# Keeping h and u in the column order of the weights, in a masked-attention kernel

## The chip, the cores and the metric

The kernel runs on one core of a Trainium2 chip. The metric is the time of one execution in device microseconds. The kernel before takes 635.86 us, the median of three runs (634.95 to 635.87). One further execution was profiled; it took 631.83 us.

## The reference

A graph of 2708 nodes has features x of [2708, 1024] and a sparse 0/1 matrix adj with about four ones in a row. All is float32.

```
h = maximum(layernorm(x), 0)
q = h @ W_q.T + b_q;  k = h @ W_k.T + b_k;  v = h @ W_v.T + b_v
z = (q @ k.T) / 32 * adj
z = where(z == 0, -10000, z)
out = x + relu(softmax(z) @ v)
```

With so few ones in a row, the kernel gathers the few rows of h that a node needs and never forms k, v or the whole of z. It uses q·k = (h M + b')·h with M = W_q.T W_k / 32, and softmax(z) @ v = u @ W_v.T + b_v with u the weighted sum of gathered rows of h.

## The kernel before

**Layouts.** The host hands W_q and W_k over with their columns permuted: position 8 m + c of a row holds input feature 128 c + m. This is the weights' column order, (m c). x, and so h, q and u, lie in natural order, (c m). A block c of 128 features is contiguous in natural order; in the weights' order its elements are 8 floats, or 32 bytes, apart. `a_tile` (L465) takes such a block out of a row of W_q as a stationary operand.

**The work in stages.** There are 22 tiles of 128 rows; the last has 20.

- To about 104 us, TensorE forms M by a Strassen-like scheme in blocks (`term`, L473 to 478). The sums lie in PSUM banks X, Y and Z, and ACT (`evicted`, L490) or VectorE (`joined`, L494, two instructions a bank) writes them to M. Both read the bank with a stride and write pieces of 64, so that M's columns are in natural order. `ts_of_m` (L438) then forms four differences T of M's quadrants on VectorE, in two parts of the columns.
- Beside it, rows of x are loaded by SP, VectorE (`bn_stats`) or ACT (`moments`) takes their statistics, GpSimd the root (L259 to 267), and ACT normalises them in place (`apply`, L276). ACT issues the store to h_dram (L283) and GpSimd adds them to hsum (L285, L298). VectorE and ACT search the rows of adj for the ones, and a counting sort orders the nodes by their number of ones. After that, work goes by sorted tiles.
- Ten units of two tiles each form q (units 0 to 9, to about 347 us), and ten units of two tiles plus a single last tile (8) form the output. A unit is seven products of 512-wide quadrants (`multiply`, L1044), each four matmuls of [128x128] by [128x512] (L1010).
- The stationary operands of a unit are blocks of the transposed rows. For rows of h, and for two tiles of u that are still in SBUF, TensorE transposes them against an identity (`half_turned`, L415), eight 128x128 blocks a tile, and ACT copies the banks out (L718). For all other rows of u, the row goes through DRAM: ACT copies u to a buffer v with pieces reordered (L944) and issues its store to u_dram, SP loads it back in four pieces of a quarter of the partitions (`by_quarters`), and VectorE turns the 32x32 blocks (`faces`, L705).
- `attention` (L959) is a stream of VectorE steps: a score for each gathered row (L863), the softmax weights, and the weighted sum u (L923). From unit 5 on it is advanced between the products of the units, by an amount of nominal time for each product (`share`, L1239 to 1242), less where the next unit has faces to turn.

**Order.** VectorE runs in the order of the program throughout, ACT until unit 4, GpSimd until unit 2. The rest is placed by the scheduler of the language.

**Row buffers.** `row_tile` (L211) hands out seven buffers of [128, 1024] in turn: for x (and h in place), for gathered rows of h, for u, for v and for rows of u loaded back. Tiles 15 to 17, and 19's companions 20 and 21, use buffers of other kinds.

```
def faces(dst, xt, lo, hi):
    return nc.vector.transpose(dst.rearrange("p c (g r) -> p g c r", r=QP),
                               xt.rearrange("p (g c r) -> p g c r", g=QUADS, r=QP)[:, :, lo:hi])
```

Of the kernel before, what the change touches and what calls it, by code (L numbers as in the profile page):

```python
# [10 lines left out]
FT = mybir.dt.float32  # L11
# [54 lines left out]
def tile_preln_masked_attention(  # L66
# [203 lines left out]
    def apply(first, only=range(4)):  # L270

        group, xs, r = normed[first]
        for i in only:
            if i < len(group):
                n = tiles[group[i]][1]
                nc.scalar.activation(xs[i][:n], xs[i][:n], AF.Relu, bias=r[:n, 4, i:i + 1], scale=r[:n, 3, i:i + 1])  # L276

# [132 lines left out]
    def half_turned(xt, s):  # L410

        pt = psum.tile([P, 4, P], FT, tag="tp", name="pt")
        for c in range(4):
            k = s * 4 + c
            nc.tensor.transpose(pt[:, c, :], xt[:, k * P:(k + 1) * P], ident)  # L415
        return pt
# [29 lines left out]
    with tc.tile_pool(name="w", bufs=1, side="left") as wp:  # L446
# [33 lines left out]
        def place(g, half, i):  # L480

            dst = M[:, g, :, i, :].rearrange("q j (c p) -> q j c p", p=P)
            pw = P // NH
            return dst[:, :, :, half * pw:(half + 1) * pw]

        def taken(bank):
            return bank.rearrange("q (p j c) -> q j c p", j=2, c=4)

        def evicted(bank, g, half, i):
            nc.scalar.activation(place(g, half, i), taken(bank), AF.Copy, scale=scale)  # L490

        def joined(bank, g, half, i):
            for j in range(2):
                nc.vector.scalar_tensor_tensor(place(g, half, i)[:, j], taken(bank)[:, j], scale,  # L494
                                               place(g, half, i)[:, j], op0=ALU.mult, op1=ALU.add)

# [89 lines left out]
        follow("i6.1-3")  # L586
        ts_of_m(0, 0)
        ts_of_m(1, 0, 1, 2, 3)
        follow("i7.0-1")
        for i in range(H):  # L590
            if i == 1:
                for half in range(NH):
                    ps = psum.tile([P, NB], FT, tag="acc", name="ps_v")
                    nc.tensor.matmul(ps, ones, acc_b[:, half * NB:(half + 1) * NB], start=True, stop=True)
                    pw = P // NH
                    nc.scalar.copy(bp_sb.rearrange("q (c p) -> q c p", c=DC)[:, :, half * pw:(half + 1) * pw],
                                   ps.rearrange("q (p c) -> q c p", c=DC))
                nc.vector.tensor_sub(bp_sb[:, NB:], bp_sb[:, NB:], bp_sb[:, :NB])
# [93 lines left out]

    faced = []

    def by_quarters(dst, rows):
# [7 lines left out]
    def faces(dst, xt, lo, hi):  # L703

        return nc.vector.transpose(dst.rearrange("p c (g r) -> p g c r", r=QP),  # L705
                                   xt.rearrange("p (g c r) -> p g c r", g=QUADS, r=QP)[:, :, lo:hi])

# [62 lines left out]
    banks_of = {0: banks_for(bp_sb)}  # L770
    ts_of_m(0, 1, 3, 2)
    follow("f8 k2 p7")
# [146 lines left out]
    def sums(t):  # L919
# [22 lines left out]
        if t in faced_tiles:  # L942
            v = row_tile(f"v_{t}")
            nc.scalar.copy(v.rearrange("p (a c r) -> p c a r", a=QUADS, r=QP),  # L944
                           u.rearrange("p (c a r) -> p c a r", a=QUADS, r=QP))
            nc.scalar.dma_start(u_dram[t * P:(t + 1) * P, :], v)
        elif near(t):
# [446 lines left out]
    with tc.If(some > 0):  # L1394
        with tc.tile_pool(name="mgen", bufs=1, side="right") as mgen:
# [6 lines left out]
            for c in range(DC):  # L1402
                mrow = mgen.tile([P, D], FT, tag="mrow", name="g_mrow", bufs=2)
                for h in range(NH):
                    ps = psum.tile([P, NB], FT, tag="acc", name="g_pm")
                    for o in range(DC):
                        nc.tensor.matmul(ps, weights_q[o].rearrange("o (p c) -> o c p", c=DC)[:, c, :],
                                         weights_k[o][:, h * NB:(h + 1) * NB], start=(o == 0), stop=(o == DC - 1))
                    pw = P // NH
                    nc.scalar.activation(mrow.rearrange("q (c p) -> q c p", c=DC)[:, :, h * pw:(h + 1) * pw],  # L1410
                                         ps.rearrange("q (p c) -> q c p", c=DC), AF.Copy, scale=scale)
                nc.sync.dma_start(m_dram[c // 4, :, :, c % 4, :].rearrange("j p w -> p j w"),
                                  mrow.rearrange("p (j w) -> p j w", j=2))
        with tc.tile_pool(name="big", bufs=1, side="right") as big, tc.tile_pool(
# [15 lines left out]
            for h in range(NH):  # L1430
                ps = psum.tile([P, NB], FT, tag="acc", name="g_c")
                nc.tensor.matmul(ps, ones, acc_c[:, h * NB:(h + 1) * NB], start=True, stop=True)
                pw = P // NH
                nc.vector.tensor_copy(c_sb.rearrange("q (c p) -> q c p", c=DC)[:, :, h * pw:(h + 1) * pw],
                                      ps.rearrange("q (p c) -> q c p", c=DC))
            bv_sb = big.tile([P, D], FT, name="bv_all")
# [3 lines left out]
            for t, (t0, n) in enumerate(tiles):  # L1440
                ht = gen.tile([P, D], FT, tag="ht", name="g_h")
                nc.sync.dma_start(ht[:n], h_dram[t0:t0 + n, :])
                for s in range(DC // 4):
                    pt = psum.tile([P, 4, P], FT, tag="tp", name="g_pt")
                    for c in range(4):
                        k = s * 4 + c
                        nc.tensor.transpose(pt[:, c, :n], ht[:n, k * P:(k + 1) * P], ident[:n, :n])
                    nc.vector.tensor_copy(hT[:, s * 4:(s + 1) * 4, t0:t0 + n], pt[:, :, :n])
            with tc.For_i(0, NT) as i:
# [5 lines left out]
                for k in range(DC):  # L1455
                    pt = psum.tile([P, 4, P], FT, tag="tp", name="g_ph")
                    nc.tensor.transpose(pt[:, 0, :], ht[:, k * P:(k + 1) * P], ident)
                    nc.vector.tensor_copy(qT[:, k, :], pt[:, 0, :])
# [22 lines left out]
                for k in range(DC):  # L1481
                    pt = psum.tile([P, 4, P], FT, tag="tp", name="g_pq")
                    nc.tensor.transpose(pt[:, 0, :], q[:, k * P:(k + 1) * P], ident)
                    nc.vector.tensor_copy(qT[:, k, :], pt[:, 0, :])
# [28 lines left out]
                for k in range(DC):  # L1513
                    pt = psum.tile([P, 4, P], FT, tag="tp", name="g_pu")
                    nc.tensor.transpose(pt[:, 0, :], u[:, k * P:(k + 1) * P], ident)
                    nc.vector.tensor_copy(qT[:, k, :], pt[:, 0, :])
# [54 lines left out]
```

## Time and profile before

| what | value |
|---|---|
| runs | 635.86 us median of 3 (634.95 to 635.87) |
| the profiled execution | 631.83 us |
| its span, from first to last instruction | 630.1 us |
| granted TensorE clock | 0.999 |
| TensorE matmul busy | 619.6 us |
| VectorE busy | 523.3 us |
| ACT busy | 288.4 us |
| GpSimd busy | 363.1 us |
| mean DMA rate | 289 GB/s |
| first matmul of the weights' product | 5.73 us |
| end of M, start of unit 0 | about 104 us |
| first face transpose | 347.9 us |

PE is TensorE's matmuls, PEld its loads of stationary operands (they run beside matmuls), DVE is VectorE, POOL is GpSimd. A group line names the line of the program, the engine, the operation, out<-in, shapes and count; then busy time and mean ns of one; then the idle time of the engine before it and what ended it. A line of a table of windows has the start and end of a stretch, its length, and then for each engine the busy time and the number of instructions, the granted clock, the share of DMA and GB/s. Matmuls are pipelined: a 128x512 matmul has two records of some 592 ns that begin 0.43 us apart.

### The profile page before, as it was taken

What the parts mean: (1) busy time and instruction counts of PE and PEld (TensorE: products, weight loads), DVE (VectorE), ACT (ScalarE), POOL (GpSimd) and SP (SyncE); (2) the same over time, 40 slices, a digit from 0 to 9 for tenths busy, and PEclk for the clock granted to TensorE, in tenths of its full rate; (3) what the DMA queues carried; (4) which work ended last, traced back from release to release, by engine and by line L of the source; (5) the groups of instructions that cost most, each with busy time, mean ns of one, the idle gap of its engine ahead of it and who ended that gap; (6) DMA issues with size and microseconds to landing.
All of it is one profiled execution on the core that took longest, in us unless ns stands there. A gap on an engine that the chain in (4) does not pass through costs nothing.

```text
span 630.1 us, 6067 instructions
## 1 busy us (share of the span) xinstructions
PE 619.6 (98%) x1579; PEld 310.3 (49%) x1579; DVE 523.3 (83%) x1022; ACT 288.4 (46%) x421; POOL 363.1 (58%) x394
## 2 busy tenths in 40 slices
PE   8999999999999999999999998999999999999996
PEld 5777766444444444454454443444444444444442
DVE  5999879997996664887988969999997999988741
ACT  3538985749677563343341333434342323343300
POOL 2649860885778177754561632757667477852241
PEclk9999999999999999999999999999999999999999
DMA  8999997688796439997489998899999999997481
GB/s 330 407 371 326 343 354 294 209 288 326 255 387 241 166 113 319 350 379 236 154 306 325 332 359 265 235 333 346 347 318 324 344 278 305 349 284 194 103 296 71
DMA packets 65088, 182.19 MB, mean 289 GB/s; under 512 B 9959, under 2 KB 20023, under 8 KB 64408
## 3 DMA queue, kind: packets, MB, share of 16 engines
q0 software_dynamic: 26656, 86.02, 43.4%
q1 hardware_dynamic: 31594, 71.53, 32.8%
q10 hardware_dynamic: 6798, 24.20, 9.8%
q8 instruction: 14, 0.23, 0.2%
q14 instruction: 26, 0.21, 0.1%
HBM read 146.70 MB, written 43.36 MB: 302 GB/s over the span
## 4 chain that ended last, share of the span: by engine, by line
PE 56%; DMA 17%; DVE 11%; issue 9%; POOL 4%; ACT 1%; SPq 1%; POOLq 0%; DVEq 0%; ACTq 0%
PE ps L1010 22%; PE psy L1010 15%; PE ps_y L476 7%; DMA out_dram<-y,tab 5%; PE ps_x L476 4%; DMA or<-u_dram 4%; PE ps_z L476 4%; DVE junk L863 4%; PE pt L415 3%; DMA pq<-q_late 2%; DVE u L923 2%; DMA q_late<-q 2%; DMA g<-h_dram,tab 2%; DMA u_dram<-v 1%; DVE a L705 1%
## 5 line engine op out<-in xcount | busy, mean ns | idle before, releaser
L1010 PE MATMUL psy<-wlow,s 128*128 128x512 f32 x320 | 144.0, 592 | 0.0
L1010 PE MATMUL ps<-M,a 128*128 128x512 f32 x320 | 144.0, 593 | 0.0
L610 POOL DMA_INDIRECT g<-h_dram,tab x91 | 110.3, 1212 | 55.8 <-ACT u L912 19.8
L863 DVE SCALAR_TENSOR_TENSOR junk<-g,pq 128x1024 uint8<-128x1024 f32 x90 | 110.0, 1223 | 16.8 <-DMA g<-h_dram,tab 10.2
L1010 PE MATMUL ps<-M,s 128*128 128x512 f32 x240 | 108.0, 592 | 2.2 <-DVE s L722 2.2
L1010 PEld LDWEIGHTS psy<-wlow,s 128*128 128x128 f32 x320 | 59.9, 190 | 72.4 <-issue 70.2
L1010 PEld LDWEIGHTS ps<-M,a 128*128 128x128 f32 x320 | 59.9, 190 | 71.8 <-issue 71.3
L923 DVE SCALAR_TENSOR_TENSOR u<-g,coef,u 128x1024 f32<-128x1024 f32 x66 | 84.6, 1282 | 4.9 <-ACT u L912 3.5
L1010 PEld LDWEIGHTS ps<-M,s 128*128 128x128 f32 x240 | 45.4, 190 | 59.7 <-issue 58.3
L389 DVE FIND_INDEX8 at<-ones,adj 128x8 uint32<-128x685 f32 (+1 forms) x88 | 74.5, 865 | 0.0
L1010 PE MATMUL psy<-wlow,a 128*128 128x512 f32 x160 | 72.0, 593 | 0.1
L368 ACT ACTIVATE sized<-adj 128x2708 uint8<-128x2708 f32 (+1 forms) x22 | 54.3, 2466 | 7.5 <-DMA adj<-in_adj_dram 6.1
L298 POOL TENSOR_TENSOR hsum<-hsum,x 128x256 f32<-128x256 f32 (+1 forms) x56 | 38.7, 728 | 25.4 <-DVE wlow L444 22.0
L1109 POOL DMA_INDIRECT y<-in_x_dram,tab x19 | 32.2, 1696 | 31.4 <-ACT y L1126 22.4
L1010 PEld LDWEIGHTS psy<-wlow,a 128*128 128x128 f32 x160 | 30.3, 190 | 38.7 <-issue 37.3
L944 ACT COPY v<-u 128x1024 f32<-128x1024 f32 x19 | 19.9, 1045 | 48.9 <-DVE u L923 43.5
L808 POOL DMA_INDIRECT out_dram<-y,tab x21 | 27.8, 1325 | 22.0 <-issue 13.6
L1010 PE MATMUL ps<-wlow,s 128*128 128x512 f32 x80 | 36.0, 592 | 0.0
L626 POOL DMA_INDIRECT tab_dram<-tab,pos_i x22 | 21.9, 993 | 20.9 <-DVE pos_i L689 15.4
L912 ACT ACTIVATE u<-g,coef 128x1024 f32<-128x1024 f32 x18 | 20.7, 1148 | 24.2 <-DVE coef L911 24.1
L760 ACT COPY ps<-bp_sb 128x512 f32<-128x512 f32 x42 | 24.6, 595 | 11.0 <-DVE y L1144 10.3
L276 ACT ACTIVATE x<-x,r 128x1024 f32<-128x1024 f32 (+1 forms) x22 | 25.8, 1232 | 5.6 <-POOL r L266 5.6
(251 smaller groups left out, 848.5 us busy)
## 6 DMA issues: line engine op xcount, KB each, us to landing
adj<-in_adj_dram SPq DMA_DIRECT2D x21, 1354.0 KB, 11.2
x<-in_x_dram SPq DMA_DIRECT2D x21, 512.0 KB, 4.2
h_dram<-x ACTq DMA_DIRECT2D x21, 512.0 KB, 8.4
u_dram<-v ACTq DMA_DIRECT2D x19, 512.0 KB, 8.5
or<-u_dram SPq DMA_DIRECT2D x76, 128.0 KB, 9.7
q_late<-q SPq DMA_DIRECT2D x12, 512.0 KB, 9.4
pq<-q_late POOLq DMA_DIRECT2D x12, 512.0 KB, 10.5
M<-in_wv_dram SPq DMA_DIRECT2D x3, 1024.0 KB, 15.4
```

The costliest lines, as they stand in the source:

```text
L276: nc.scalar.activation(xs[i][:n], xs[i][:n], AF.Relu, bias=r[:n, 4, i:i + 1], scale=r[:n, 3, i:i + 1])
L298: small.append(nc.gpsimd.tensor_add(hsum[:n, cols], hsum[:n, cols], xt[:n, cols]))
L368: nc.scalar.activation(sized[:n], a[:n, :, :PW], AF.Abs, accum_out=total[:n, t:t + 1])
L389: nc.vector.max_index(at[:n, k - first_k, g, :], ones[:n, 0:8], a[:n, g, :])
L476: mm = nc.tensor.matmul(bank, a_tile(o + H * a[0], a[1], i), b(o), start=first and o == 0, stop=(o == H - 1), skip_group_check=True)
L610: return nc.gpsimd.indirect_dma_start(out=dst, out_offset=None, in_=src, in_offset=off, bounds_check=N - 1, oob_is_err=False)
L760: nc.scalar.copy(return_[h], row[:, h * NB:(h + 1) * NB])
L808: to = nc.gpsimd.indirect_dma_start(out=out, out_offset=bass.IndirectOffsetOnAxis(ap=ptab.bitcast(U32)[:n, t, SLOTS:SLOTS + 1], axis=0), i ...
L863: chained(lambda: nc.vector.scalar_tensor_tensor(junk, g_of[t][s], 1.0, tq[t], op0=ALU.mult, op1=ALU.mult, accum_out=zall[:, t, s:s + 1]))
L923: chained(lambda: nc.vector.scalar_tensor_tensor(u, g_of[t][s], coef[:, s:s + 1], u, op0=ALU.mult, op1=ALU.add))
L1010: mm = nc.tensor.matmul(bank, a[:, c, :], b[:, c, :], start=False, stop=(c == 3), skip_group_check=True)
L1109: return nc.gpsimd.indirect_dma_start(out=y[:n], out_offset=None, in_=x, in_offset=off, compute_op=ALU.add)
```

## The change

h, q, u and the columns of M are all in the weights' column order.

- **Normalisation** writes its result in the order (m c), and so no longer in place: a spare eighth buffer takes the first result, and the raw buffer just read becomes the spare for the next.
- **M's blocks** are written as the banks hold them. `joined` is one instruction a bank instead of two. The biases' copies are plain as well. `ts_of_m` cuts T by quadrant and not by columns: six of its eight subtractions stand ahead of unit 0 (five before), two behind its first transposes (three before).
- **u** is stored as it was summed. The copy to v and the buffer v are gone.
- **The transposes** take the blocks with a stride of 8 floats: `half_turned` on TensorE, `faces` on VectorE.
- **Row buffers** are seven tiles held by hand and dealt out in turn, with a table that says which x goes to which; the eighth lives as long as the search of adj.

The rest of the diff changes a fallback path in the same way; it isn't entered for this input.

```diff
+    rows7 = [work.tile([P, D], FT, name=f"row{i}", bufs=1) for i in range(ROWS)]
+    extra = edge.tile([P, D], FT, name="row_extra")
+    x_place = dict(zip((11, 12, 13, 14, 18, 19, 0), range(7))) | {1: None, 2: 0, 3: 1, 4: 2, 5: 3, 6: 4, 7: 5, 8: 6, 9: 0, 10: 1}
+    spare, turn_of, faced = [extra], [1], []
     def row_tile(name):
-        return work.tile([P, D], FT, tag="row", name=name, bufs=ROWS)
+        turn_of[0] += 1
+        row = rows7[(turn_of[0] - 1) % ROWS]
+        faced[:] = [y for y in faced if y is not row]
+        return row
...
-                xt = row_tile(f"x_{t}")
-            if t < EARLY:
-                kept[t] = xt
+                xt = extra if x_place[t] is None else rows7[x_place[t]]
...
-        for i in only:
+        for i in (1, 2, 0) if first == FULL - 2 else only:
             if i < len(group):
                 n = tiles[group[i]][1]
-                nc.scalar.activation(xs[i][:n], xs[i][:n], AF.Relu, bias=r[:n, 4, i:i + 1], scale=r[:n, 3, i:i + 1])
+                ht = spare.pop()
+                nc.scalar.activation(ht[:n].rearrange("p (m c) -> p c m", c=DC), xs[i][:n].rearrange("p (c m) -> p c m", c=DC),
+                                     AF.Relu, bias=r[:n, 4, i:i + 1], scale=r[:n, 3, i:i + 1])
+                spare.append(xs[i])
+                xs[i] = ht
+                if group[i] < EARLY:
+                    kept[group[i]] = ht
...
-            k = s * 4 + c
-            nc.tensor.transpose(pt[:, c, :], xt[:, k * P:(k + 1) * P], ident)
+            nc.tensor.transpose(pt[:, c, :], xt.rearrange("p (m c) -> p c m", c=DC)[:, s * 4 + c], ident)
...
-        cut = slice(part * (P // NH), (part + 1) * (P // NH))
-        m = [[M[:, i, j].rearrange("p c (b w) -> p (c b) w", w=P)[:, :, cut] for j in range(2)] for i in range(2)]
-        t = [T[:, k].rearrange("p c (b w) -> p (c b) w", w=P)[:, :, cut] for k in range(4)]
+        cut = slice(2 * part, 2 * part + 2)
+        m = [[M[:, i, j, cut] for j in range(2)] for i in range(2)]
+        t = [T[:, k, cut] for k in range(4)]
...
         def place(g, half, i):
-            dst = M[:, g, :, i, :].rearrange("q j (c p) -> q j c p", p=P)
-            pw = P // NH
-            return dst[:, :, :, half * pw:(half + 1) * pw]
-        def taken(bank):
-            return bank.rearrange("q (p j c) -> q j c p", j=2, c=4)
+            return M[:, g, half, i]
         def evicted(bank, g, half, i):
-            nc.scalar.activation(place(g, half, i), taken(bank), AF.Copy, scale=scale)
+            nc.scalar.activation(place(g, half, i), bank, AF.Copy, scale=scale)
         def joined(bank, g, half, i):
-            for j in range(2):
-                nc.vector.scalar_tensor_tensor(place(g, half, i)[:, j], taken(bank)[:, j], scale,
-                                               place(g, half, i)[:, j], op0=ALU.mult, op1=ALU.add)
+            nc.vector.scalar_tensor_tensor(place(g, half, i), bank, scale, place(g, half, i), op0=ALU.mult, op1=ALU.add)
...
-        ts_of_m(0, 0)
-        ts_of_m(1, 0, 1, 2, 3)
+        ts_of_m(0, 0, 1, 2)
+        ts_of_m(1, 0, 1, 2)
...
-                                   xt.rearrange("p (g c r) -> p g c r", g=QUADS, r=QP)[:, :, lo:hi])
+                                   xt.rearrange("p (g r c) -> p g c r", g=QUADS, r=QP)[:, :, lo:hi])
...
-    ts_of_m(0, 1, 3, 2)
+    ts_of_m(0, 3)
+    ts_of_m(1, 3)
...
-            v = row_tile(f"v_{t}")
-            nc.scalar.copy(v.rearrange("p (a c r) -> p c a r", a=QUADS, r=QP),
-                           u.rearrange("p (c a r) -> p c a r", a=QUADS, r=QP))
-            nc.scalar.dma_start(u_dram[t * P:(t + 1) * P, :], v)
+            nc.scalar.dma_start(u_dram[t * P:(t + 1) * P, :], u)
```

More of the change, by code (lines that the diff above doesn't have):

```diff
@@ L691, in tile_preln_masked_attention @@
     behind = []
-    faced = []
     def by_quarters(dst, rows):
@@ L1446, in tile_preln_masked_attention @@
                         k = s * 4 + c
-                        nc.tensor.transpose(pt[:, c, :n], ht[:n, k * P:(k + 1) * P], ident[:n, :n])
+                        nc.tensor.transpose(pt[:, c, :n], ht[:n].rearrange("p (m c) -> p c m", c=DC)[:, k], ident[:n, :n])
                     nc.vector.tensor_copy(hT[:, s * 4:(s + 1) * 4, t0:t0 + n], pt[:, :, :n])
@@ L1456, in tile_preln_masked_attention @@
                     pt = psum.tile([P, 4, P], FT, tag="tp", name="g_ph")
-                    nc.tensor.transpose(pt[:, 0, :], ht[:, k * P:(k + 1) * P], ident)
+                    nc.tensor.transpose(pt[:, 0, :], ht.rearrange("p (m c) -> p c m", c=DC)[:, k], ident)
                     nc.vector.tensor_copy(qT[:, k, :], pt[:, 0, :])
@@ L1482, in tile_preln_masked_attention @@
                     pt = psum.tile([P, 4, P], FT, tag="tp", name="g_pq")
-                    nc.tensor.transpose(pt[:, 0, :], q[:, k * P:(k + 1) * P], ident)
+                    nc.tensor.transpose(pt[:, 0, :], q[:, :D].rearrange("p (m c) -> p c m", c=DC)[:, k], ident)
                     nc.vector.tensor_copy(qT[:, k, :], pt[:, 0, :])
@@ L1514, in tile_preln_masked_attention @@
                     pt = psum.tile([P, 4, P], FT, tag="tp", name="g_pu")
-                    nc.tensor.transpose(pt[:, 0, :], u[:, k * P:(k + 1) * P], ident)
+                    nc.tensor.transpose(pt[:, 0, :], u[:, :D].rearrange("p (m c) -> p c m", c=DC)[:, k], ident)
                     nc.vector.tensor_copy(qT[:, k, :], pt[:, 0, :])
```

12 lines of the change are left out of this document (3 added, 9 removed).

## The prediction

> **What bounds the kernel now.** I read the page first, then the waits of TensorE, then a table of windows by stage, and last the groups by shape of the engines whose access patterns change.
>
> ```profile
> span 630.1 us, 6067 instructions
> PE 619.6 (98%) x1579; PEld 310.3 (49%) x1579; DVE 523.3 (83%) x1022; ACT 288.4 (46%) x421; POOL 363.1 (58%) x394
> ```
>
> ```profile
> PE ps L1010 <- DVE s L722: 2.2, 1, 2.2
> PE ps_y L511 <- POOL hsum L121: 1.2, 1, 1.2
> PE ps L1010 <- DVE T_alone L705: 0.8, 1, 0.8
> PE ps_x L476 <- DMA wlow<-in_wq_dram: 0.6, 1, 0.6
> ```
>
> TensorE is busy 98% of the span and waits for others four times, 4.8 us in all. So it is the bound almost everywhere. Two things follow. Whatever shortens work of another engine can give back at most these 4.8 us. And whatever makes TensorE's own work longer adds to the time one to one.
>
> ```profile
> 5.70:103.90 98.20, 98.17 (x230) 71.16 (x231) 86.17 (x176) 64.27 (x82) 55.70 (x69) 1.00 0.97 367
> 103.90:154.40 50.50, 50.50 (x158) 25.04 (x157) 43.77 (x123) 37.54 (x51) 34.12 (x58) 1.00 0.73 255
> 373.00:398.00 25.00, 22.84 (x54) 9.98 (x53) 24.09 (x44) 8.12 (x15) 6.40 (x5) 1.00 0.86 279
> 398.00:424.00 26.00, 26.00 (x62) 11.41 (x62) 25.44 (x42) 10.47 (x17) 16.60 (x16) 1.00 0.99 304
> 424.00:450.00 26.00, 26.00 (x62) 11.58 (x61) 25.39 (x43) 11.40 (x18) 18.88 (x15) 1.00 1.05 340
> 450.00:476.00 26.00, 26.00 (x62) 11.48 (x61) 24.06 (x42) 10.34 (x17) 17.90 (x13) 1.00 1.05 330
> 502.00:528.00 26.00, 26.00 (x68) 11.97 (x67) 24.30 (x44) 10.27 (x18) 20.57 (x15) 1.00 0.95 297
> ```
>
> The columns are the length of the window, then the busy time of PE, PEld, DVE, ACT and POOL. The first two rows are the product of the weights and the first units of q. There ACT has 34 and 13 us to spare. The others lie in the output units (from about 347 us): ACT is busy for less than half, VectorE for 24.1 of 25, 25.4 of 26, 25.4 of 26. VectorE is the second bound there, with 0.6 us to spare in 26 at its tightest.
>
> **The change, part by part: TensorE's transposes.** Rows of h and u now lie in the order (m c), so the block that `half_turned` takes for one transpose has its 128 elements 8 floats (32 bytes) apart. It was contiguous. In TensorE's rows the program's names stand with the moving operand first (`psy<-wlow,s` is s stationary, T moving), so `pt<-ident,x` loads the data as weights and streams the identity. What changes is a weight load.
>
> ```profile
> L415 PEld LDWEIGHTS pt<-ident,qr 128*128 128x128 f32 x96 | 11.2, 141 | 5.8 <-issue 5.6 <-DVE g L1262 0.2
> L1010 PEld LDWEIGHTS ps<-M,a 128*128 128x128 f32 x320 | 59.9, 190 | 71.8 <-issue 71.3 <-ACT ps L760 0.5
> L476 PEld LDWEIGHTS ps_y<-wlow 128*128 128x128 f32 x64 | 20.1, 313 | 7.4
> ```
>
> ```profile
> 103.90:347.00 243.10, 20.63 (x160) 18.31 (x159) 1.00 0.77 268
> 347.00:606.00 259.00, 2.07 (x16) 1.87 (x16) 1.00 0.95 295
> ```
>
> ```profile
> 103.89 0.25 PEld L415 LDWEIGHTS pt<-ident,x 128*128 128x128 f32 x2
> 104.00 0.25 PEld L415 LDWEIGHTS pt<-ident,x 128*128 128x128 f32 x2
> 124.13 0.87 PE pt L415 x8
> ```
>
> The kernel before already has a weight load of exactly the new pattern: `a_tile` (L465) takes every eighth float of a row of the weights. It needs 313 ns where the contiguous load of the same shape and type (L1010) needs 190, that is 123 ns more. That costs nothing at L476, where one matmul of 512 columns covers the next load. At L415 nothing covers it: eight transposes take 0.87 us, 109 ns each, and the loads (the timeline's windows) begin 0.11 us apart and last 141 ns, so each already runs 32 ns past the start of the next. With 123 ns more a load takes 264 ns and the spacing becomes 264 - 32 = 232 ns, 123 more per transpose. There are 160 + 16 of them (the windows of L415), in 22 batches of 8, one per tile. The first load of a batch still lies under a long matmul, so 154 pay: 154 x 0.123 = 18.9 us, straight onto TensorE. Were the load stretched in proportion instead (141 x 313/190 = 232, spacing 200), it would be 154 x 0.091 = 14.0. If the first ones paid too, 176 x 0.123 = 21.6. A gain is excluded: the spacing of 109 is already the streaming of 128 columns at the rate of the matmuls. I take 18.9, since the 123 ns are seen on the same 128 x 128 floats.
>
> The Trainium skill's page "TensorE: Matmul & The Clock Gate", section "LDWEIGHTS (loading the stationary operand)", lets a load's time depend on its columns alone (columns / 1.2 in ns); by that this term is nothing and the sum falls to the VectorE term below. The rows of L476 and L1010 have the same 128 columns and differ by 123 ns, so the trace speaks against it; it keeps a part of rival D.
>
> **VectorE's face transposes.** `faces` turns 32 x 32 blocks of the u rows. Its input had runs of 32 floats and now has a stride of 8. The DMAs of `by_quarters` stay as they are, pieces of 1 KB.
>
> ```profile
> L705 DVE STREAM_TRANSPOSE a<-or 128x512 f32<-128x512 f32 x28 | 18.6, 693 | 0.0
> L705 DVE STREAM_TRANSPOSE s<-or 128x512 f32<-128x512 f32 x8 | 5.3, 669 | 0.0
> L705 DVE STREAM_TRANSPOSE T_alone<-or 128x1024 f32<-128x1024 f32 x1 | 1.2, 1246 | 10.6 <-DMA or<-u_dram 10.6
> L662 DVE TENSOR_REDUCE bad<-sort 128x14 f32<-128x224 f32 x1 | 0.4, 386 | 0.0
> L688 DVE TENSOR_REDUCE deg<-sort 128x8 f32<-128x144 f32 x1 | 0.4, 420 | 0.0
> L662 DVE TENSOR_REDUCE bad<-sort 128x8 f32<-128x128 f32 x1 | 0.3, 285 | 0.0
> ```
>
> No transpose before reads such a stride, but one reduction does: L688 in its form of 8 tiles runs over "p (d t) -> p t d", a step of 8 floats. Contiguous reductions cost 285 ns at 128 elements and 386 at 224, 1.05 ns each, so 144 would take 302. The strided one takes 420: 118 / 144 = 0.82 ns more per element. For 512 elements that is 0.42 us per transpose, for the 36 of them 15.1 us, for T_alone 0.84. The ends are 0 (only reductions pay) and 15.1 (all on the path); less than 0 isn't possible, as the 693 ns hold no stall that a stride would take away. What of it shows depends on VectorE's room. Each window of the table holds 4 faces (1.7 us), that from 424 to 450 six (2.5 us). 24.09 + 1.7 is 0.8 over 25, 25.44 + 1.7 is 1.1 over 26, 25.39 + 2.5 is 1.9 over 26. The others stay within their lengths. So 3.8 us come out; VectorE runs in program order, and TensorE waits behind it for the operands of the next unit.
>
> The Trainium skill has two rules for this. "VectorE: DVE Perf Modes", section "Mode 1× (REGULAR) — the baseline", has fp32 and odd strides run at one result a cycle, by which the term is 0 and the sum 18.9 (rival B). "SBUF — State Buffer", in its note on cachelines under "Door 1: The DMA port swizzle", charges every access that enters a new line of 16 bytes, which a step of 32 always does. L688 sides with the second.
>
> **The copy of u (L944).**
>
> ```profile
> L944 ACT COPY v<-u 128x1024 f32<-128x1024 f32 x19 | 19.9, 1045 | 48.9 <-DVE u L923 43.5 <-DVE u L929 5.3
> L276 ACT ACTIVATE x<-x,r 128x1024 f32<-128x1024 f32 x21 | 24.7, 1232 | 5.6 <-POOL r L266 5.6
> ```
>
> Nineteen copies go, 19.9 us of ACT, where ACT is idle more than half the time: nothing. The store of u is still issued by ACT after the last sum, so the queue behind it is held as before, only 1.05 us less. On a path the 1.05 us stand once: the last tile (8) goes through u_dram to T_alone, for which TensorE waits 0.8 us. There 1.05 less and 0.84 more for the slower turn leave -0.2 us. One row buffer per tile instead of two means buffers come free no later. As TensorE waits for no row buffer, that gives nothing.
>
> **Normalisation, L276.** It now writes with a stride of 8 floats into another buffer. No row shows ACT writing so. The bounds are 0 and, by the ratio 313/190 of the strided load, 0.8 us for each of 22, 18 us of ACT. ACT has 34 and 13 us spare in the two windows where they lie, 15 and 7 of the 22 applied there and after; the cover holds even at the upper end, so 0 in the sum, and up to 2 in the range for an eviction that comes late. The spare buffer is always the raw one that the previous step has just read on ACT itself: no wait is added. SP's x loads wait for the store and sum of another h tile of the same group, but for x_10, which waits for h_4 instead of h_3; that one has been turned by the start of unit 1, and x_10 is asked for late in it: nothing again.
>
> **M, T and the biases.**
>
> ```profile
> L490 ACT ACTIVATE M<-ps_y 128x512 f32<-128x512 f32 x8 | 4.7, 594 | 8.6 <-PE ps_y L476 8.6
> L494 DVE SCALAR_TENSOR_TENSOR M<-ps_y,M 128x256 f32<-128x256 f32 x8 | 2.8, 413 | 0.0
> L1144 DVE SCALAR_TENSOR_TENSOR y<-psy,y 128x512 f32<-128x512 f32 x1 | 0.7, 692 | 2.5 <-PE psy L1010 2.5
> L444 DVE TENSOR_TENSOR wlow<-M 128x1024 f32<-128x1024 f32 x4 | 4.8, 1213 | 0.0
> ```
>
> Sixteen joins of 413 ns become eight of about 692, -1.1 us of VectorE in a stage with 12 us of room and no wait on TensorE. The 16 evictions stay, with plain patterns. The eight subtractions stay eight of 1.2 us; six come ahead of unit 0 instead of five, two after instead of three. All of it 0. Without that cover the moved one would cost 1.2 us.
>
> **Sum:** 18.9 + 3.8 - 0.2 = 22.5 us. The profiled execution took 631.83 us (630.1 of span and 1.7 around it) and would become 654.3. The runs' median is 635.86, 4.0 above that execution, so there the forecast is 658.4 us (A).
>
> **The rivals.** About 0.2% (1.3 us) is what a measurement of this kernel can tell from no change.
>
> B, TensorE pays, VectorE doesn't: the stride costs the 32 x 32 turn nothing, and the last wait is 1.05 us shorter, of which 0.8 count. 635.86 + 18.9 - 0.8 = 654.0. For it: only a reduction shows a strided price on VectorE. Against: it is the same read of the same memory.
>
> C, VectorE pays, TensorE doesn't: loads run further ahead than one. 635.86 + 3.8 - 0.2 = 639.5. Against: loads begin 0.11 us apart, one for each streaming matmul, and none begins two ahead.
>
> D, no slower: a load for a transpose (141 ns against 190 for a matmul) is a form of its own that goes by columns alone, and the turn likewise. Its place is L415, its price 0, and it decides as soon as the strided load adds less than 8 ns (154 x 8 ns is 1.3 us). What is left is the shorter way to T_alone: 635.86 - 0.8 = 635.1; with the 2.2 us wait at L722 gone as well, 632.9. For it: the 313 ns are seen on loads for matmuls only.
>
> E, everything on the path: VectorE's backlog can't be made good, 21.6 + 15.1 + 0.8 = 37.5, so 673.
>
> **How the numbers follow.** A 0.50, B 0.22, C 0.08, D 0.16, E 0.04. The forecast is that of A. A reaches from 14.0 to 18.9 plus 13 of VectorE and late evictions, 650 to 668; B from 649 to 657. The range 639 to 668 holds A, B and the middle of C and leaves out D and E. D splits into 0.07 faster and 0.09 within 0.2%; A, B, C and E are slower, 0.84.
>
> **What would show it.** Right: weight loads of L415 near 264 ns, eight transposes in 1.7 to 1.9 us and not 0.87, the q units (104 to 347 us) about 17 us longer; L705 near 1.1 us, new waits of TensorE on L705 or L722 between 373 and 450 us; L944 gone, with no change that one can see from it. Wrong: 0.87 us for eight transposes (C or D), or L705 at 0.69 (B). If the loads are long and the span isn't, my reading of TensorE as the bound fails. If ACT's normalisation takes over 2 us and TensorE waits on evictions around 90 to 125 us, I have the wrong cover.

## The result, and the profile after

The kernel after takes 655.3 us, the median of four runs (654.49 to 656.76), beside 635.87 us for the kernel before (634.95 to 636.9): 1.0308 times as long, 95% interval 1.0283 to 1.0333. The forecast of 658.4 was 3.1 us too high. The sum was nearly right and its largest term was not, as the profile shows at once. The profiled execution took 655.76 us. First the page of the kernel after, then the waits of TensorE.

```profile
span 654.1 us, 6045 instructions
PE 628.1 (96%) x1579; PEld 314.3 (48%) x1579; DVE 537.0 (82%) x1014; ACT 292.3 (45%) x402; POOL 363.3 (56%) x394
...
PEclk9999997999999999999999999999999999999978
```

```profile
PE pt L426 <- ACT M L496: 5.1, 2, 4.8
PE ps L1008 <- DVE T_alone L705: 4.2, 1, 4.2
PE psy L1008 <- ACT psy L1021: 2.9, 2, 2.5
PE ps L1008 <- DVE s L722: 2.9, 2, 1.9
PE psy L1008 <- DVE q L1089: 1.6, 1, 1.6
PE psy L1008 <- ACT u L1052: 1.4, 2, 0.9
```

The span grew by 24.0 us, 4.6 more than the 19.4 of the runs: the one profiled execution of the kernel before was 4.0 us faster than its median, and that of the kernel after 0.5 slower. So some of each difference between the two traces is not the change's. TensorE's busy time grew by 8.5 us only. It waits some 20 us where it waited 4.8 (the six largest entries stand here). The largest waits are for ACT at the end of M and for the last turn on VectorE, and at just these two places the granted clock dips (the 7 in the seventh slice and the one near the end).

The groups by shape that answer to those of before (L426 is the old L415, L283 the old L276, L499 the old L494):

```profile
L426 PEld LDWEIGHTS pt<-ident,row 128*128 128x128 f32 x168 | 22.8, 193 | 15.5 <-issue 7.9 <-ACT M L496 6.2 <-PE ps L1008 1.1
L283 ACT ACTIVATE row<-row,r 128x1024 f32<-128x1024 f32 x12 | 27.2, 2266 | 0.3
L705 DVE STREAM_TRANSPOSE a<-row 128x512 f32<-128x512 f32 x28 | 29.7, 1087 | 0.3 <-DMA u_dram<-row 0.3
L705 DVE STREAM_TRANSPOSE s<-row 128x512 f32<-128x512 f32 x8 | 8.5, 1062 | 0.0
L705 DVE STREAM_TRANSPOSE T_alone<-row 128x1024 f32<-128x1024 f32 x1 | 2.0, 2005 | 11.2 <-DMA row<-u_dram 11.2
L499 DVE SCALAR_TENSOR_TENSOR M<-ps_y,M 128x512 f32<-128x512 f32 x4 | 2.5, 676 | 0.0
```

The turns rose from 693 to 1087 ns, as forecast (0.42 us more; it is 0.39). The normalisation went from 1232 to 2266 ns, 1.03 us more and above the 0.8 that I gave as the upper end. The weight load of a transpose went from 141 to 193 ns and not to 264. A piece of the chain of waits shows what eight of them cost:

```profile
216.51 0.88 PE pt L426 x8
```

That is 0.11 us each, the spacing of before. Loads now run 84 ns past the start of the next one, and the transposes come no later for it.

The place of the loss can be read from the start of one product in each unit, s2 by T1, in the two traces:

| unit | before, us | after, us | difference |
|---|---|---|---|
| 0 | 113.55 | 121.47 | +7.9 |
| 2 | 165.46 | 173.42 | +8.0 |
| 4 | 217.15 | 228.59 | +11.4 |
| 9 | 346.92 | 358.49 | +11.6 |
| 11 | 397.38 | 409.57 | +12.2 |
| 14 | 469.48 | 484.36 | +14.9 |
| 17 | 542.72 | 558.49 | +15.8 |
| 19 | 591.66 | 609.60 | +17.9 |
| last product of unit 19 | 610.11 | 634.06 | +24.0 |

7.9 us are lost before unit 0 starts, 3.5 more by unit 4, of which 2.5 are the wait for ACT at L1021. From unit 4 to 9, where 9 tiles (72 blocks) go through TensorE's transposes, 0.1 us is lost. From there to unit 19 it is 6.4, in the tail 6.0. (The last product of unit 9 ends at 371 us in the trace of before; 347 us is only the start of its third one.)

How the first loss comes about is in the timeline of TensorE at the end of M, and that of the tail in the second piece:

```profile
93.44 10.46 PE L487 MATMUL ps_y<-wk,wq 128*128 128x512 f32 x24
108.69 1.12 PE L426 MATMUL pt<-ident,row 128*128 128x128 f32 x4 [4.79 <-ACT M L496]
110.15 2.83 PE L426 MATMUL pt<-ident,row 128*128 128x128 f32 x12 [0.34 <-ACT M L496]
```

```profile
619.90 3.60 PE L1008 MATMUL psy<-wlow,s 128*128 128x512 f32 x8
627.66 6.56 PE L1008 MATMUL ps<-M,T_alone 128*128 128x512 f32 x8 [4.17 <-DVE T_alone L705]
634.06 3.60 PE L1008 MATMUL psy<-wlow,a 128*128 128x512 f32 x8
```

M is done at 103.9, but the transposes of unit 0 need the banks of Y, and ACT evicts the first of the last four only at 108.06 (94.72 before). The lines of ACT, from before and from after:

```profile
94.72 0.57 ACT L490 ACTIVATE M<-ps_y 128x512 f32<-128x512 f32 x1
```

```profile
108.06 0.57 ACT L496 ACTIVATE M<-ps_y 128x512 f32<-128x512 f32 x1
```

Then twelve transposes take 2.83 us, where 0.11 each would make 1.3, and in the tail four matmuls (eight records) take 6.56 us and not 3.70. A table of windows gives the reason in its clock column (length, PE busy, granted clock):

```profile
104.38:107.79 3.41, 0.00 (x0) 1.00 0.84 330
107.80:114.60 6.80, 5.57 (x26) 0.50 0.71 261
623.21:626.62 3.41, 0.28 (x1) 1.00 1.07 332
626.63:633.44 6.81, 5.78 (x7) 0.50 0.91 309
```

The clock falls to a half within each of the two long waits, 0.9 and 1.0 us before its end, and stays there for 6.8 us. So 5.9 and 5.8 us of work run at half clock, which costs up to 3.0 and 2.9 us on top of the wait. The Trainium skill's page "TensorE: Matmul & The Clock Gate", section "Why this matters for your kernels", warns of gaps over about 3 us; by that rule both waits, 4.8 and 4.2 us, halve the clock, and the trace agrees. But a wait of 3.3 us in a run below leaves the clock alone, and shorter ones in others halve it, so the length of the wait does not decide by itself.

### The profile page after: what moved, and what is told of

It is laid out like the page before. It is cut to its first block, busy times and chain, and to the rows that moved or that the text cites. A ratio compares the mean times of both kernels' runs of the same rounds, so it can differ in the third digit from the quotient of the medians.

```text
span 654.1 us, 6045 instructions
## 1 busy us (share of the span) xinstructions
PE 628.1 (96%) x1579; PEld 314.3 (48%) x1579; DVE 537.0 (82%) x1014; ACT 292.3 (45%) x402; POOL 363.3 (56%) x394
## 4 chain that ended last, share of the span: by engine, by line
PE 22%; DVE 21%; DMA 17%; issue 16%; ACT 14%; POOL 7%; another core or an unknown queue 1%; ACTq 1%; SPq 0%; POOLq 0%; DVEq 0%
PE ps L1008 12%; PE psy L1008 8%; DVE row L924 5%; DMA row<-u_dram 5%; DVE junk L864 4%; ACT row L283 4%; DMA g<-h_dram,tab 3%; ACT sized L380 3%; DVE a L705 3%; DMA u_dram<-row 3%; POOL g L612 2%; POOL hsum L310 2%; ACT x L283 2%; PE pt L426 2%; DMA row<-in_x_dram 2%
## 5 line engine op out<-in xcount | busy, mean ns | idle before, releaser
L924 DVE SCALAR_TENSOR_TENSOR row<-g,coef,row 128x1024 f32<-128x1024 f32 x66 | 84.5, 1280 | 3.8 <-ACT row L913 2.4
L913 ACT ACTIVATE row<-g,coef 128x1024 f32<-128x1024 f32 x18 | 20.7, 1152 | 34.5 <-DVE coef L912 26.7
L809 POOL DMA_INDIRECT out_dram<-y,tab x20 | 25.6, 1282 | 15.2 <-issue 13.3
L310 POOL TENSOR_TENSOR hsum<-hsum,row 128x256 f32<-128x256 f32 x44 | 30.4, 731 | 3.8 <-DVE keys L420 3.1
L426 PEld LDWEIGHTS pt<-ident,row 128*128 128x128 f32 x168 | 22.8, 193 | 15.5 <-issue 7.9
L705 DVE STREAM_TRANSPOSE a<-row 128x512 f32<-128x512 f32 x28 | 29.7, 1087 | 0.3 <-DMA u_dram<-row 0.3
```

The source lines that it names most:

```text
L310: small.append(nc.gpsimd.tensor_add(hsum[:n, cols], hsum[:n, cols], xt[:n, cols]))
L426: nc.tensor.transpose(pt[:, c, :], xt.rearrange("p (m c) -> p c m", c=DC)[:, s * 4 + c], ident)
L809: to = nc.gpsimd.indirect_dma_start(out=out, out_offset=bass.IndirectOffsetOnAxis(ap=ptab.bitcast(U32)[:n, t, SLOTS:SLOTS + 1], axis=0), i ...
L924: chained(lambda: nc.vector.scalar_tensor_tensor(u, g_of[t][s], coef[:, s:s + 1], u, op0=ALU.mult, op1=ALU.add))
```

## The experiments

Each was timed beside the kernel before on its own chip, so the differences count and not the plain times.

| kernel | us | before, us | difference | ratio (95%) |
|---|---|---|---|---|
| after | 655.30 | 635.87 | +19.4 | 1.0308 (1.0283 to 1.0333) |
| before, strided transposes | 635.87 | 634.88 | +1.0 | 1.0016 (0.9989 to 1.0043) |
| after, plain normalisation | 647.77 | 634.88 | +12.9 | 1.0208 (1.0167 to 1.0249) |
| after, plain turns | 640.26 | 634.88 | +5.4 | 1.0093 (1.0072 to 1.0114) |
| after, normalisation reads with a stride | 655.00 | 634.88 | +20.1 | 1.0333 (1.0309 to 1.0357) |
| after, both plain | 628.13 | 633.71 | -5.6 | 0.9912 (0.9895 to 0.9928) |
| after, matmuls in the last gap | 648.20 | 633.71 | +14.5 | 1.0228 (1.0211 to 1.0245) |
| after, copy of u on ACT | 641.36 | 633.71 | +7.7 | 1.0117 (1.0100 to 1.0134) |
| before, buffers by hand | 636.44 | 635.56 | +0.9 | 1.0009 (0.9984 to 1.0035) |
| weights in face order | 631.89 | 635.75 | -3.9 | 0.9942 (0.9920 to 0.9964) |

**Does TensorE pay?**

```diff
-            k = s * 4 + c
-            nc.tensor.transpose(pt[:, c, :], xt[:, k * P:(k + 1) * P], ident)
+            nc.tensor.transpose(pt[:, c, :], xt.rearrange("p (m c) -> p c m", c=DC)[:, s * 4 + c], ident)
```

> The kernel before, with one part of the change: the transposes on TensorE take their blocks with a stride of 8 floats. Rows keep their natural order, so q is formed from features in another order; the work is the same. The recorded theory (a strided load of weights spaces the transposes 0.23 us apart) expects +18.9 us, 654.8, and eight transposes in 1.7 us or more. The theory formed on the profile after (the load gets longer, 0.19 us, but the spacing stays 0.11 us) expects no change, 635.9 within 1.3 us, and eight transposes in 0.87 us.

The time is that of before; the interval ends at 1.0043, 2.7 us, where the recorded term is 18.9. The groups and the chain of waits of this kernel:

```profile
L414 PEld LDWEIGHTS pt<-ident,qr 128*128 128x128 f32 x96 | 12.4, 191 | 7.8 <-issue 7.5 <-DVE g L1261 0.2
```

```profile
244.84 0.89 PE pt L414 x8
```

A load of 191 ns, 50 longer, and eight transposes in 0.89 us, where it was 0.87. The recorded theory of this term falls.

**Does the normalisation pay, and why?**

```diff
-                nc.scalar.activation(ht[:n].rearrange("p (m c) -> p c m", c=DC), xs[i][:n].rearrange("p (c m) -> p c m", c=DC),
-                                     AF.Relu, bias=r[:n, 4, i:i + 1], scale=r[:n, 3, i:i + 1])
+                nc.scalar.activation(ht[:n], xs[i][:n], AF.Relu, bias=r[:n, 4, i:i + 1], scale=r[:n, 3, i:i + 1])
```

> The kernel after, but the normalisation writes its rows contiguously, in natural order, so q and the scores mix features; everything else as after. Theory N (the strided write of the normalisation makes ACT late, evictions of M come late, TensorE waits and its clock drops) expects the 11.6 us that are lost by unit 9 to go, 643.7, with L283 near 1.23 us. The recorded theory expects 2 us at most, 653 or more, since ACT had cover.

L283 falls to 1241 ns, the wait for the evictions and the first drop of the clock are gone, and unit 0 stands where it stood before (113.52).

```profile
L283 ACT ACTIVATE row<-row,r 128x1024 f32<-128x1024 f32 x12 | 14.9, 1241 | 0.3
```

6.5 us are won against the difference of after (19.4 to 12.9), not 11.6: in the profile of this kernel 4.4 us are lost between units 3 and 4, where TensorE waits 2.7 us for gathered rows and its clock halves for 3.4 us. That wait is 0.3 us in the kernel after. So theory N holds for the first loss; how much of the 11.6 us it explains, this run alone doesn't say. The largest waits of TensorE in it:

```profile
PE ps L1007 <- DVE T_alone L704: 3.9, 1, 3.9
PE ps L1007 <- DVE s L721: 2.9, 2, 1.9
PE pt L425 <- DMA row<-h_dram,tab: 2.7, 1, 2.7
```

**Is it the write?**

```diff
-                nc.scalar.activation(ht[:n].rearrange("p (m c) -> p c m", c=DC), xs[i][:n].rearrange("p (c m) -> p c m", c=DC),
+                nc.scalar.activation(ht[:n].rearrange("p (m c) -> p m c", c=DC), xs[i][:n].rearrange("p (c m) -> p m c", c=DC),
```

> The kernel after, but the normalisation runs through its elements in the order of its output: it writes contiguously and reads with a stride of 128 floats. Nothing is left out. If only a strided write is dear on ACT, 643.7 us as with a plain normalisation, L283 near 1.23 us. If a strided read costs as much, 655.

It takes 655.0, L283 2195 ns. ACT pays nearly as much for a strided read from SBUF as for a strided write. So neither of the two orders tried, contiguous on one side and strided on the other, is free on ACT.

```profile
L283 ACT ACTIVATE row<-row,r 128x1024 f32<-128x1024 f32 x12 | 26.3, 2195 | 0.3
```

Its tail holds a fact on the clock. TensorE waits 3.3 us for T_alone, and the clock does not fall:

```profile
627.78 3.70 PE L1008 MATMUL ps<-M,T_alone 128*128 128x512 f32 x8 [3.30 <-DVE T_alone L705]
```

```profile
622.74:626.16 3.42, 1.74 (x5) 1.00 1.09 381
626.16:629.57 3.41, 1.79 (x4) 1.00 0.99 264
```

In all twelve traces the stretches of full and of half clock follow a grid of 3.41 us, and every fall within the work comes at the end of a piece of that grid in which TensorE was busy for 0.44 of the time or less (none at all and 0.08 of it in the two drops of the kernel after). Here the wait lies across two pieces, busy for 0.51 and 0.52 of it, and so a wait of 3.3 us leaves the clock alone.

**Do the turns pay?**

```diff
-                                   xt.rearrange("p (g r c) -> p g c r", g=QUADS, r=QP)[:, :, lo:hi])
+                                   xt.rearrange("p (g c r) -> p g c r", g=QUADS, r=QP)[:, :, lo:hi])
```

> The kernel after, but the 32 x 32 turns on VectorE read runs of 32 floats as before, so the output multiplies features in another order. If the turns' strided read is what is lost from unit 9 on (6.4 us to unit 19 and 6.0 in the tail), 643 us, with L705 near 0.69 us and no drop of the clock in the tail. If the backlog of the first stage is carried into the output units instead, 653 or more.

It takes 640.26: 14.0 us less of a difference than after, more than the 12.4 that the table of starts shows from unit 9 on. By its profile this kernel does not merely lose nothing after unit 9, it wins 3.1 us against the one before: a gain that the stride had covered. TensorE waits for T_alone no longer, and the clock drops once only, at the end of M, where the slow normalisation still is.

```profile
L705 DVE STREAM_TRANSPOSE a<-row 128x512 f32<-128x512 f32 x28 | 18.6, 692 | 0.3 <-issue 0.3
```

**What is the rest of the change worth?** Both edits together.

> The kernel after with both the normalisation and the turns on VectorE plain, so features are mixed up on the way; the strided loads of TensorE, the plain blocks of M, the missing copies of u and the buffers stay. If the strides of ACT and VectorE are all that the change loses, 635 or less, down to 632, since from unit 9 on the kernel with plain turns was 3.1 us faster than the one before. If something else costs (the buffers by hand, the order of T), 637 or more.

628.13 us, 5.6 less than before. TensorE has only the two waits of the start left:

```profile
PE ps_y L514 <- POOL hsum L121: 1.2, 1, 1.2
PE ps_x L486 <- DMA wlow<-in_wq_dram: 0.6, 1, 0.6
```

So the change has a gain of its own, and the two strides take it back several times over. From this base the turns' stride alone costs 18.5 us (-5.6 to +12.9), the normalisation's alone 11.0 (-5.6 to +5.4), both together 25.0. They seem to overlap by 4.5. But the kernel with strided turns alone, from which the 18.5 comes, is the one that loses 4.4 us between units 3 and 4 in its profile, near 204 us, long before its first turn at 354. Up to there its code is that of the kernel with both plain, which loses nothing there. So that part is no price of the turns. Without it they would cost some 14.1 from this base (an estimate, as 18.5 is from the runs and 4.4 from one trace), which is the 14.0 found with the strided normalisation, and the two prices would simply add up.

The four runs of the kernel with both plain lie within 0.35 us, at granted clocks of 0.998 and 0.999. The seven of the kernel before beside them spread over 1.7 us, at 0.996 to 0.998. So a part of the gain may be drops of the clock that the kernel before has in some executions; no trace shows them.

**Does the last wait cost the clock?**

```diff
+            warm = psum.tile([P, NB], FT, tag="tp", name="warm")
+            for _ in range(4):
+                nc.tensor.matmul(warm, ones, hsum[:, :NB], start=True, stop=True)
             single["first"] = one_started(single["banks"], single["turned"][:, 0:4, :])
```

> The kernel after, with four matmuls of 128x512 into a bank that nobody reads, ahead of the first product of the last tile, where TensorE waits 4.2 us for T_alone; nothing is left out. If that wait makes the clock drop to half for 6.8 us, the drop in the tail is gone and 3.4 us with it: 651.9. If the clock falls for another reason, 655.3 and the drop stays.

The difference falls by 4.9 us, to +14.5. The timeline of TensorE:

```profile
618.56 3.60 PE L1032 MATMUL warm<-hsum,ones 128*128 128x512 f32 x8
622.47 3.70 PE L1008 MATMUL ps<-M,T_alone 128*128 128x512 f32 x8 [0.32 <-DVE T_alone L705]
```

The gap is filled, and the first product of T_alone takes 3.70 us and not 6.56; there is no drop in the tail. That part, some 2.9 us, is shown. The other 2 us lie elsewhere in the profile (the wait for ACT around 200 us is 0.4 and not 2.5 us, though the normalisation is as slow, and the first drop is 3.4 us long and not 6.8) and aren't explained by the edit.

**Which strides cost?** Normalisations of four patterns on lines of their own, and every other turn at half the stride. This kernel ran once (643.49 us) and is read for durations alone:

```diff
+                if w == 1:
+                    nc.scalar.activation(to.rearrange("p (b k w) -> p b k w", k=8, w=2)[:, :, :, 0].rearrange("p b k -> p (b k)"), at[:, :NB], AF.Relu, bias=bias, scale=by)
...
+                    nc.scalar.activation(to.rearrange("p (m c w) -> p c m w", c=DC, w=2), at.rearrange("p (c m w) -> p c m w", c=DC, w=2), AF.Relu, bias=bias, scale=by)
...
+            return nc.vector.transpose(dst.rearrange("p c (g r) -> p g c r", r=QP),
+                                       xt[:, lo * P:hi * P].rearrange("p (g r c) -> p g c r", g=QUADS, r=QP))
```

> One look for durations; the kernel after, with normalisations of four patterns in turn (two halves written with a stride of 2 floats; runs of 2, of 4, of 8 floats, 8 runs apart) and every other turn of VectorE at a stride of 4 floats and not 8, so features are mixed up. If ACT and VectorE pay for each new piece of 16 bytes, a stride of 2 and runs of 4 and 8 take 1.23 us for 1024 elements (two halves of 0.65) and runs of 2 nearly so, and a turn with a stride of 4 still pays, near 1.09. If they pay by the step between elements, runs of 2 take about 1.75 us, of 4 about 1.5, and the turn at a stride of 4 is between 0.69 and 1.09.

The groups of this kernel by shape: L287 writes every second float (512 elements), L290, L292 and L294 write runs of 2, 4 and 8; L719 turns at a stride of 4, L721 at 8.

```profile
L287 ACT ACTIVATE row<-row,r 128x512 f32<-128x512 f32 x4 | 3.5, 872 | 1.6 <-POOL r L272 1.5
L290 ACT ACTIVATE row<-row,r 128x1024 f32<-128x1024 f32 x3 | 3.8, 1280 | 0.1
L292 ACT ACTIVATE row<-row,r 128x1024 f32<-128x1024 f32 x3 | 3.7, 1240 | 0.1
L294 ACT ACTIVATE row<-row,r 128x1024 f32<-128x1024 f32 x2 | 2.5, 1241 | 0.1
L719 DVE STREAM_TRANSPOSE a<-row 128x512 f32<-128x512 f32 x18 | 19.8, 1099 | 0.3 <-DMA u_dram<-row 0.3
L721 DVE STREAM_TRANSPOSE s<-row 128x512 f32<-128x512 f32 x8 | 8.5, 1068 | 0.0
```

Runs of 2 floats are already all but free on ACT (1280 ns beside 1240). Single floats two apart cost 872 ns for 512, where the contiguous Relu of 512 in the trace of before (L1126) takes 631: 0.47 ns more per element, against 1.01 at a step of 8. A turn pays as much at a step of 4 floats as at 8. Neither theory had all of this. The Trainium skill's page "SBUF — State Buffer", in the note on cachelines under "Door 1: The DMA port swizzle", wants two hits on each 16 bytes; runs of 2 agree, while a step of 2 floats also has two and still pays 0.47 ns.

**Is VectorE the wrong place for the reordering?**

```diff
-            nc.scalar.dma_start(u_dram[t * P:(t + 1) * P, :], u)
+            v = row_tile(f"v_{t}")
+            nc.scalar.copy(v.rearrange("p (a c r) -> p a c r", a=QUADS, r=QP), u.rearrange("p (a r c) -> p a c r", a=QUADS, r=QP))
+            nc.scalar.dma_start(u_dram[t * P:(t + 1) * P, :], v)
```

with plain turns.

> The kernel after, with the reordering copy of u back on ACT (it now reads with a stride of 8 floats) and plain turns on VectorE; nothing is left out. If the turns' stride costs because VectorE is full while ACT has room, the copy of some 2.2 us is hidden and the time is that of plain turns, 640 to 643. If the stride costs as much wherever it lies, 652 or more.

641.36 us, +7.7 beside +5.4 with plain turns and no copy. The copies take 2073 ns each, 39.4 us of ACT, and some 2.3 us of it show; the intervals of the two ratios overlap.

```profile
L945 ACT COPY row<-row 128x1024 f32<-128x1024 f32 x19 | 39.4, 2073 | 44.6 <-DVE row L924 38.3 <-DVE row L930 5.6 <-DMA pq<-q_dram,tab 0.7
```

The same reordering on VectorE took 14.9 us of it (36 turns by 0.39 and T_alone by 0.76) and cost 14.0 over plain turns.

**Where does the gain come from?** The buffers alone, in the kernel before: `rows7`, `extra`, `x_place` and the normalisation out of place, contiguous.

> The kernel before with one part of the change alone: the row buffers dealt out by hand, with the normalisation out of place but contiguous; all orders of columns, the copies of u and the turns are those of before, and nothing is left out. The kernels with plain turns lose no time between units 10 and 11 where the kernel before waits (about 2.3 us), and two of them share only the buffers and the plain M with each other. If the buffers do that, 631 to 632 us, faster than both kernels; if it is the plain blocks of M or the missing copies of u, no change, 634 to 635.

636.44, no change that can be told. In its profile the wait between units 10 and 11 is indeed gone (the difference to before falls from +3.9 to +1.5), but 3.8 us are lost between units 3 and 4, to the same gathered rows as above.

```profile
202.84 1.06 PE L426 MATMUL pt<-ident,row 128*128 128x128 f32 x8 [1.93 <-DMA row<-h_dram,tab]
```

The twelve runs of this kernel spread from 631.44 to 640.37. The kernel with strided transposes, whose time is that of before too, loses 2.5 us at the same place, while the one trace of before shows no such wait. What sets off that wait is open.

**A layout without the strides.** If the columns of W_q and W_k come as (a c r), feature 128 c + 32 a + r at position 256 a + 32 c + r, the normalisation writes runs of 32, TensorE's blocks are contiguous, u needs no copy and the turns read runs of 32:

```diff
-                nc.scalar.activation(ht[:n].rearrange("p (m c) -> p c m", c=DC), xs[i][:n].rearrange("p (c m) -> p c m", c=DC),
+                nc.scalar.activation(ht[:n].rearrange("p (a c r) -> p c a r", c=DC, r=QP),
+                                     xs[i][:n].rearrange("p (c a r) -> p c a r", c=DC, r=QP),
...
-            return wq_sb[o].rearrange("o (p c) -> o c p", c=DC)[:, H * high + i, :]
+            return wq_sb[o][:, (H * high + i) * P:(H * high + i + 1) * P]
...
-            held[t] = u
+            held[t] = row_tile(f"n_{t}")
+            nc.scalar.copy(held[t].rearrange("p (c a r) -> p c a r", c=DC, r=QP), u.rearrange("p (a c r) -> p c a r", c=DC, r=QP))
...
+    def faced(w):
+        w = np.asarray(w)
+        return w.reshape(-1, D8, QUADS, QP).transpose(0, 2, 1, 3).reshape(-1, P, D8, 1)
```

> A kernel of its own, with nothing left out: the host hands W_q and W_k over with their columns in the order (a c r), feature 128 c + 32 a + r at position 256 a + 32 c + r, and h, q, u and M's columns lie in that order. The normalisation then writes runs of 32 floats, the blocks that TensorE transposes and those of W_q are contiguous, u is stored as summed, and the turns on VectorE read runs of 32. The two tiles of u that stay in SBUF get a copy to natural order on ACT. If the strides are the whole loss and the rest of the change is worth what the kernel with both strides plain showed (5.6 us), 629 to 631 us, faster than both kernels by 0.6% or more. If that gain came from the mixed features and not from the layout, 635.

631.89 us, 0.9942 of before (0.9920 to 0.9964): faster than both kernels. In its profile L283 takes 1241 ns, L706 692, and there is no wait for ACT or T_alone. It stays 1.7 us behind the kernel with both strides plain, by the differences, though the intervals touch; its profile has 1.7 us of the gathered rows' wait:

```profile
PE pt L428 <- DMA row<-h_dram,tab: 1.7, 1, 1.7
PE ps_y L516 <- POOL hsum L121: 1.2, 1, 1.2
PE psy L1010 <- DVE m L904: 0.8, 1, 0.8
PE ps_x L488 <- DMA wlow<-in_wq_dram: 0.2, 1, 0.2
```

## Why the prediction was right, and where it wasn't

The direction was right, and strides were the reason. That the size fits is luck: 18.9 of the 22.5 us forecast stood on TensorE's transposes, which measured 1.0 us (-0.7 to 2.7), and two terms that were far too small, the turns and the normalisation, made it up. Rival B's 654.0 is nearer still to the 655.3 measured, and its account (TensorE pays, VectorE doesn't) is the wrong way round.

- *TensorE is the bound, and other engines' gains give back at most the 4.8 us of waits.* Roughly right. With both strides plain the waits fell by 3 us and the profiled span by 3.8; the runs say 5.6.
- *A strided load takes 264 ns and spaces the transposes 232 ns apart, 18.9 us.* This step failed. The load takes 191 to 193 ns, and the spacing is 0.11 us as before, shown in the kernel before by that edit alone; the sign that I had given against it, 0.87 us for eight transposes, is what came. The error was to take the recorded length of a load, less a fixed 32 ns, for the time that keeps the next one off. Rival C was right on this point. The Trainium skill's rule by columns alone gives the right term, 0, though the load itself is 52 ns longer.
- *VectorE pays 0.42 us a turn.* Right: 0.39, from a single reduction with the same stride.
- *Of that, 3.8 us show, and the tail gains 0.2.* This failed by its size. By the table of starts 6.4 us are lost in the output units and 6.0 in the tail, and taking the stride away gives 14.0. The rooms of 26 us windows were added up as if each could be filled to the end, and the tail was costed for its own turn and the missing copy alone. TensorE waits 4.2 us for T_alone and not 0.8. Of the 3.4 us more, 2.1 are VectorE's lag (its last sum of u ends at 613.4 and not 593.4, 20.0 us later, where TensorE is 17.9 behind) and 0.8 the longer turn; and the way from that sum through DRAM to the turn takes 12.23 us and not 11.65, longer although a copy of 1.05 is gone from it. Then the clock halves. The 14.0 is close to the 14.9 us that the turns take longer, as in the VectorE part of rival E, but some 2.9 of it are the clock's.
- *The normalisation costs ACT at most 0.8 us each and the cover holds.* This failed twice. It is 1.03 us, and the cover of 34 us was not room ahead of the evictions: 22.8 us of it lie before 47.2 us, ahead of the first normalisation, and from there to the eviction at 94.7 ACT had 4.7 us to spare. Fifteen normalisations of 1.03 us more (15.5 us) had to fit there, and pushed that eviction to 108.1. The sign that I had given for it (over 2 us, TensorE waiting on evictions between 90 and 125 us) is what came.
- *The missing copies, the joins and the buffers are worth nothing.* Too low: together with the plain order of M they are worth 5.6 us, once nothing covers them. Which of them is not settled; the buffers alone don't show it in the time.
- *What was not there at all:* the clock. Two waits of over 4 us cost some 3 us each beside themselves; for the one in the tail, filling the gap shows it.

From a base of -5.6, +11.0 for the normalisation and then +14.0 for the turns make the +19.4 measured; the forecast had +18.9 for TensorE, +3.8 for the turns and -0.2.

## What to carry to other kernels

A layout change moves a stride from one engine to another; before it is made, ask which engine reads or writes single elements afterwards, and measure there, since TensorE's weight loads took this stride at no cost in time while ACT and VectorE took 57 to 84% longer for an instruction. Room on an engine counts only up to the instruction that others wait for: look for its idle time ahead of that one, not in the whole stage. And an engine that is nearly full, as VectorE was here with 0.6 us to spare in 26, carries a lag into the end of the kernel, where nothing hides it.

## What the runs showed of the hardware

- The recorded load of a stationary 128x128 block of floats at a step of 8 floats takes 191 ns for a transpose (141 contiguous) and 313 for a matmul (190 in the face order, the same loads without the step). The transposes kept their 0.11 us with loads of 0.19.
- ACT takes 2266 ns to write 1024 floats at a step of 8, 2195 to read them at a step of 128, and 1241 for both sides contiguous; runs of 2 floats are enough for 1280.
- The 32 x 32 turn takes 1087 ns for 512 elements at a step of 8 floats and 1099 at a step of 4, 693 with runs of 32.
- TensorE's clock halves for 3.4 or 6.8 us around a wait, and the wait's length alone doesn't say whether: it did for waits of 4.8, 4.2 and 2.7 us, for one of 2.05 us (with the copy of u on ACT) and one of 1.93 (buffers by hand); it didn't for one of 3.3 us (strided read) and one of 2.5 (the kernel after). What parts them in the twelve traces is the busy share of the piece of 3.41 us that holds the wait, on the grid on which the clock changes: all 23 pieces at full clock that a fall follows, those at the kernels' ends included, have 0.436 or less, and every other piece at full clock has 0.443 or more. So where a wait lies on that grid decides, too.
